# A fused graph, attention and expert kernel on one core: a fourth last group into the output, denominators copied out by ScalarE, x in halves and idle transposes at the start

## The chip, the cores and the metric

The kernel runs on one core of one Trainium2 chip. The metric is the device time of one execution in microseconds (us); lower is better. A core has five engines with a queue each: TensorE (PE in the profile, its weight loads PEld), VectorE (DVE), ScalarE (ACT), GpSimd (POOL) and SyncE (SP), and DMA engines that all queues share. Each engine works its own list of instructions in order and waits on semaphores for the others.

## The reference

With x of 4096 tokens by 256 features and a dense 4096 by 4096 matrix adj, all in float32, cut to what matters:

```python
h = layernorm(x)
x = x + concat([h, (adj @ (h @ neigh_W.T)) / (adj.sum(1) + 1)]) @ lin_W.T
f = layernorm(x)
q, k, v = rope(rmsnorm(f) @ wq.T), rope(rmsnorm(f) @ wk.T), rmsnorm(f) @ wv.T   # 4 heads, 2 kv heads
f2 = f + softmax(causal(q @ k.T / 8)) @ v @ wo.T
flat = rmsnorm(f2)
w = top-2 of softmax(flat @ router_w.T), scaled to sum 1                          # 8 experts
x = x + f2 + sum_e w[:, e] * (silu(flat @ w1[e].T) * (flat @ w3[e].T)) @ w2[e].T
```

## The kernel before, in words

The tokens lie in 8 blocks (`NB`) of 4 tiles (`TB`) of 128. There are three stages, and the order of the instructions on each engine is the order in which the program writes them.

**Graph stage** (L217 to L528). Block 0 of x is loaded first (L238), then the weights `neigh_w` and half of `lin_t` on SP's queue (L241, L242), with the other half on ACT's (L245), then more of x and the first blocks of adj. `scales_x(0)` takes mean and variance of the block (`stats`, L153: four `bn_stats`, four `bn_aggr` on VectorE) and the inverse deviation (`power`, L161: two POOL operations). `normed_x` normalizes one tile on VectorE (L172). `fold` (L279) multiplies the two weights on TensorE into `ml_sb`; `turned_x(0)` transposes the block on TensorE (L319), and `features(0)` (L386) multiplies the two. Then `aggregate` runs over the blocks of adj (L424), with features and later q, k, v as steps in between.

**Attention stage** (L532 to L1337). The list `runs` (L1276) goes over blocks in `ORDER`, two head pairs p, and four key tiles at a time. A run has two places for other work, `place_for_steps(2n)` after the next run's scores and `place_for_steps(2n + 1)` after its own values. `scores` puts two products into one of three PSUM pairs of banks, and ScalarE takes the exponential (L561). `totals` sums the probabilities on VectorE (L579), and `values` multiplies them by v (L591). When a block and head pair is done, `unload` copies the accumulator by ScalarE (L598), and `normalize` (L600) sums over keys by a product with ones into `den`, takes the reciprocal on VectorE (L609) and multiplies (L610). `den` lies in the pool `p_ms`, which has one bank: the next user of it (`project` L625, `turn` L644, `logits`, `weigh`, `place`, `rotate` of the last block) waits until it is read. `at` (L1279) gives each step that needs this bank a place of its own, noted in `taken`; steps that begin with None share a place. For each `normalize` the place after it is put into `taken` as well (L1301). `after(b)` (L800) lists what follows a block: projection, transposes, router, and scatters of its rows into `lists` by expert.

**Expert stage** (L1339 to L1354). Tokens are sorted by expert into 25 whole groups of 256 rows (`NW`) and small groups of 128, of which 17 always run: 42 in all (`NM`). `TURNS` (L55) sets their order: nine whole ones, then whole and small interleaved, then the last `LAST` whole ones. In iteration k: `hidden(k)` (L1176), the load `load13(k + 3)`, `combine(k - 1)`, then `load_rows(k + 4)` and `load2(k + 2)`, all loads on SP. From k = 6, whole groups but the last two are combined by seven smaller products (L1147), for which `split` (L1102) prepares sums of the hidden units and of `w2` on VectorE. Each half of a group is added to its tokens' rows by an indirect DMA with addition from POOL (L1248): into `acc_dram` for the first groups, into `out` for the last `LAST`. At k = NM - LAST, SP copies `acc_dram` into `out` (L1349); it waits for all adds into `acc_dram`, and the adds into `out` wait for it. Adds of different groups into one tensor wait for each other. `load_rows(k + 4)` reuses the buffer of group k - 1 and so waits for that group's add.

Of the kernel before, what the change touches and what calls it, by code (L numbers as in the profile page):

```python
# [9 lines left out]
F32 = mybir.dt.float32  # L10
# [3 lines left out]
ALU = mybir.AluOpType  # L14
# [3 lines left out]
P = 128  # L18
N = 4096
C = 256  # L20
NB = 8
TB = 4
# [9 lines left out]
EPS_LN = 1e-5  # L32
# [16 lines left out]


ALONE = 9
LAST = 3
RARE = 4
NM = NG - RARE
TURNS = list(range(ALONE)) + [  # L55
# [1 line left out]
        ((g - first + 0.5) / (end - first), g)  # L57
        for first, end in ((ALONE, NW - LAST), (NW, NM)) for g in range(first, end)
    )
] + list(range(NW - LAST, NW)) + list(range(NM, NG))  # L60
PADS = 512 + SM
# [5 lines left out]
def fast_kernel(  # L67
# [24 lines left out]
    nc = tc.nc  # L92
# [4 lines left out]
    ident = const.tile([P, P], F32, name="ident")  # L97
# [20 lines left out]
    half = const.tile([P, TB, 1], F32, name="half")  # L118
    nc.gpsimd.memset(half, -0.5)
    experts = const.tile([P, TB, NE], F32, name="experts")  # L120
    for e in range(NE):
# [15 lines left out]
    res = [  # L137
        res_all[:, b * TB * C : (b + 1) * TB * C].rearrange("p (t c) -> p t c", t=TB)
        for b in range(NB)
    ]  # L140
# [5 lines left out]
    mv = [const.tile([P, TB, 2], F32, name=f"mv{b}") for b in range(NB)]  # L146
    rstd = [const.tile([P, TB, 1], F32, name=f"rstd{b}") for b in range(NB)]
    both = [const.tile([P, TB, 1], F32, name=f"both{b}") for b in range(NB)]

    x_blocks = x.rearrange("(b t p) c -> b p t c", t=TB, p=P)  # L150
    out_blocks = out.rearrange("(b t p) c -> b p t c", t=TB, p=P)

    def stats(pool, b):  # L153

        st = pool.tile([P, TB, nc.vector.BN_STATS_DIM], F32, tag="st", name=f"st_{b}")
        for t in range(TB):
            nc.vector.bn_stats(st[:, t, :], res[b][:, t, :])
        for t in range(TB):
            nc.vector.bn_aggr(mv[b][:, t, :], st[:, t, :])

    def power(dst, src, scale, eps):  # L161

        nc.gpsimd.tensor_scalar(dst, src, scale, eps, op0=ALU.mult, op1=ALU.add)
        nc.gpsimd.tensor_tensor(dst, dst, half, op=ALU.pow)

# [4 lines left out]
    def normed(dst, b, t, scale):  # L170

        nc.vector.tensor_scalar(  # L172
            dst, res[b][:, t, :], mv[b][:, t, 0:1], scale, op0=ALU.subtract, op1=ALU.mult
        )
# [42 lines left out]
    with (  # L217
# [11 lines left out]
        def load_x(b):  # L229
            nc.sync.dma_start(res[b], x_blocks[b])  # L230

        def load(n):

            if n < NB * NB:
                blocks[n] = adjs.tile([P, TB, 512], F32, tag="a", name=f"a_{n // NB}_{n % NB}")
                nc.sync.dma_start(blocks[n], adj[n // NB, n % NB])

        load_x(0)  # L238

        wn_sb, l2_sb = qT[4][:, :, 0:C], qT[5][:, :, 0:C]  # L240
        nc.sync.dma_start(wn_sb, neigh_w.rearrange("(c p) o -> p c o", p=P))  # L241
        nc.sync.dma_start(l2_sb, lin_t[C : 2 * C, :].rearrange("(c p) o -> p c o", p=P))  # L242

        ml_sb = qT[6]
        nc.scalar.dma_start(  # L245
# [33 lines left out]
        def fold():  # L279
            for c in range(2):  # L280
                pm = p_pj.tile([P, 512], F32, tag="pj", name=f"pm_{c}")
                for k in range(2):
                    nc.tensor.matmul(
                        pm[:, :C], wn_sb[:, k, c * P : (c + 1) * P], l2_sb[:, k, :],
                        start=(k == 0), stop=(k == 1),
                    )
                nc.scalar.copy(ml_sb[:, c, 0:C], pm[:, :C])
# [43 lines left out]

        inputs, turned = {}, {}

        def scales_x(b):
            stats(gx, b)
            power(rstd[b], mv[b][:, :, 1:2], 1.0, EPS_LN)
            nc.gpsimd.memset(g[b][:, G22 : T1 + 1, :, HC : HC + 1], 1.0)

        def normed_x(b, t):
            if t == 0:  # L340
                inputs[b] = gx.tile([P, TB, C], F32, tag="f", name=f"f_{b}", bufs=1)
            normed(inputs[b][:, t, :], b, t, rstd[b][:, t])
# [119 lines left out]
        def qkv(b):  # L462
# [3 lines left out]
            def scales():  # L466
                stats(gx, b)
                var = mv[b][:, :, 1:2]
                power(both[b], var, *BOTH)
                power(rstd[b], var, 1.0, EPS_LN)  # L470
# [33 lines left out]

        scales_x(0)
        for t in range(TB):
            normed_x(0, t)
        fold()  # L510
        load(2)
        for b in range(6, NB):
            load_x(b)
        scales_x(1)
        turned_x(0)
        features(0)
        turned_x(1)
        scales_x(2)
        steps = {jb: [] for jb in range(NB)}
        for jb in range(NB):  # L520
# [11 lines left out]
    with (  # L532
# [67 lines left out]
        def normalize(b, p):  # L600
            den = p_ms.tile([P, 512], F32, tag="ms", name=f"dn_{b}_{p}")
            total = sums.pop((b, p))
            for j in range(2):
                nc.tensor.matmul(
                    den[j * HD : (j + 1) * HD, :], ones[:, 0:HD], total[:, j, :],
                    start=True, stop=True,
                )
            rden = ax.tile([P, 512], F32, tag="rden", name=f"rden_{b}_{p}")
            nc.vector.reciprocal(rden, den)  # L609
            nc.vector.tensor_mul(ys[b, p], ys[b, p], rden)  # L610


# [210 lines left out]
        def last_qkv():  # L823
            b, made = NB - 1, {}

            def scales():
                stats(ax, b)
                var = mv[b][:, :, 1:2]
                power(rstd[b], var, 1.0, EPS_LN)
                power(both[b], var, *BOTH)  # L830
# [370 lines left out]
        def combine(k):  # L1201
# [33 lines left out]
            for h in range(n):  # L1235
# [6 lines left out]
                else:  # L1242
# [5 lines left out]
                put = nc.gpsimd.indirect_dma_start(  # L1248
                    out=(acc_dram if k < NM - LAST else out)[:, :],
                    out_offset=at,  # L1250
# [26 lines left out]
        later, taken = {}, set()  # L1277

        def at(n, steps):  # L1279

            for fs in steps:
                if fs[0] is None:
                    fs = fs[1:]
                else:
                    while n in taken:
                        n += 1
                    taken.add(n)
                later.setdefault(n, []).extend(fs)
                n += 1
            return n  # L1290
# [6 lines left out]
        ends = {}  # L1297
        for n, (b, p, s) in enumerate(runs[:-1]):
            if s == TB * b:
                ends[b, p] = at(2 * n + 3, [[lambda b=b, p=p: normalize(b, p)]])  # L1300
                taken.add(ends[b, p])  # L1301
        at(0, last_qkv())
        end = 0
        for b in ORDER[:-1]:
# [7 lines left out]
        for n, (b, p, s) in enumerate(runs):  # L1312
# [15 lines left out]


        rest = [[lambda: normalize(ORDER[-1], 1)]] + after(ORDER[-1]) + [  # L1330
            [lambda: make_table(NB, True, NA, NW - NA)], [lambda: make_table(NB, False, NW, NG - NW)],
        ]
        rest = iter([fs for fs in ([f for f in fs if f] for fs in rest) if fs])

        def step():
            for f in next(rest, []):
                f()  # L1337

        load13(2)  # L1339
        for k in range(NM):  # L1340
# [4 lines left out]
            if k:  # L1345
                combine(k - 1)
                step()
            if k == NM - LAST:
                nc.sync.dma_start(out, acc_dram[0:N, :])  # L1349
# [656 lines left out]
@with_exitstack  # L2006
def adj_ffn_kernel(ctx: ExitStack, tc: tile.TileContext, *args):
    nc = tc.nc
    kept = ctx.enter_context(tc.tile_pool(name="kept", bufs=1))
    left_over = kept.tile([1, 1], I32, name="left_over")  # L2010
    table = kept.tile([P, 2, RARE], I32, name="rare_table")
    mine = kept.tile([P, RARE, NE], F32, name="rare_mine")
    lists = fast_kernel(tc, *args, left_over, table, mine)
    state = nc.values_load(left_over[0:1, 0:1], min_val=0, max_val=2)
    with tc.If(state != 0):  # L2015
        with tc.If(state == 2):
            general_kernel(tc, *args)
# [76 lines left out]
```

## Time and profile before

| | |
|---|---|
| median of 3 runs | 1620.64 us (1619.17 to 1621.63) |
| profiled execution | 1620.5 us span |
| graph stage | 0 to about 555 us |
| attention stage | about 555 to 1105 us |
| expert stage | about 1105 us to the end |
| VectorE busy, 580 to 1020 us | 358.0 of 440 us |
| ScalarE busy, 580 to 1020 us | 226.8 of 440 us |
| last product of TensorE ends | 1606.4 us |

In the profile, L12 is line 12 of the program before. A line of a timeline gives the start, the duration, the engine, the line, the operation, what is written and read, the count, and in brackets how long the engine idled before it and what ended that. A q behind an engine's name means its sequencer, such as one that issues a DMA. TensorE is busy nearly all the time, so the places where it isn't are what to look at:

```profile
0.00:20.00 20.00, 12.50 (x38) 1.00 0.94 329
...
700.00:800.00 100.00, 98.01 (x501) 1.00 0.06 22
800.00:900.00 100.00, 97.39 (x494) 1.00 0.09 33
900.00:1000.00 100.00, 99.81 (x483) 1.00 0.08 28
```

These are stretches of the span with TensorE's busy time in each (the columns: stretch, length, busy time and count, granted clock, share of the DMA engines, GB/s).

### The profile page before, as it was taken

What the parts mean: (1) busy time and instruction counts of PE and PEld (TensorE: products, weight loads), DVE (VectorE), ACT (ScalarE), POOL (GpSimd) and SP (SyncE); (2) the same over time, 40 slices, a digit from 0 to 9 for tenths busy, and PEclk for the clock granted to TensorE, in tenths of its full rate; (3) what the DMA queues carried; (4) which work ended last, traced back from release to release, by engine and by line L of the source; (5) the groups of instructions that cost most, each with busy time, mean ns of one, the idle gap of its engine ahead of it and who ended that gap; (6) DMA issues with size and microseconds to landing.
All of it is one profiled execution on the core that took longest, in us unless ns stands there. A gap on an engine that the chain in (4) does not pass through costs nothing. (4 is left out here: it accounts for less than half of the span.)

```text
span 1620.5 us, 25640 instructions
## 1 busy us (share of the span) xinstructions
PE 1592.0 (98%) x9894; PEld 1159.0 (72%) x9894; DVE 1014.8 (63%) x2135; ACT 480.9 (30%) x917; POOL 403.4 (25%) x604
## 2 busy tenths in 40 slices
PE   8999999999999999999999999999999999999996
PEld 5779999999999544344343433437889999999995
DVE  5656756756665678778878888793445444443541
ACT  2110100100100445555454455553212222222221
POOL 1001111112112230443434323322422212222222
PEclk9999999999999999999999999999999999999998
DMA  6324434444444000000001000057756777777775
GB/s 227 97 75 142 157 131 160 138 139 148 160 134 134 4 0 1 24 31 28 35 20 40 28 13 28 17 186 230 236 165 200 240 231 243 251 244 215 242 238 149
DMA packets 67716, 209.79 MB, mean 129 GB/s; under 512 B 14656, under 2 KB 46272, under 8 KB 53952
## 3 DMA queue, kind: packets, MB, share of 16 engines
q1 hardware_dynamic: 54592, 190.32, 34.7%
q0 software_dynamic: 12720, 17.47, 5.4%
q8 instruction: 80, 1.31, 0.3%
q14 instruction: 52, 0.43, 0.1%
q10 hardware_dynamic: 272, 0.26, 0.0%
HBM read 180.81 MB, written 31.42 MB: 131 GB/s over the span
## 5 line engine op out<-in xcount | busy, mean ns | idle before, releaser
L561 ACT ACTIVATE pt<-sc 128x1024 f32<-128x1024 f32 (+3 forms) x288 | 251.6, 958 | 201.3 <-PE sc L556 167.1
L579 DVE TENSOR_TENSOR sum<-sum,pt 128x1024 f32<-128x1024 f32 (+3 forms) x258 | 293.7, 1138 | 20.6 <-POOL pt L563 0.5
L424 PE MATMUL acc<-g,a 128*128 128x128 f32 x2048 | 255.7, 275 | 0.0
L556 PE MATMUL sc<-qT_all,kT 64*128 64x512 f32 (+3 forms) x1152 | 251.4, 570 | 2.8 <-ACT pt L561 1.9
L591 PE MATMUL ya<-pt,vv 128*64 128x512 f32 (+3 forms) x1152 | 242.6, 563 | 0.0
L424 PEld LDWEIGHTS acc<-g,a 128*128 128x128 f32 x2048 | 241.8, 192 | 0.0
L1176 PE MATMUL h<-xT,qT_all 128*128 128x256 f32 (+1 forms) x1232 | 216.6, 335 | 0.0
L1176 PEld LDWEIGHTS h<-xT,qT_all 128*128 128x128 f32 x1232 | 193.4, 191 | 19.0 <-issue 1.0
L556 PEld LDWEIGHTS sc<-qT_all,kT 64*128 64x128 f32 x1152 | 103.5, 186 | 138.2 <-issue 103.0
L1183 DVE TENSOR_TENSOR hT<-si,h 128x256 f32<-128x256 f32 (+2 forms) x126 | 62.6, 506 | 190.6 <-ACT si L1182 190.5
L591 PEld LDWEIGHTS ya<-pt,vv 128*64 128x64 f32 x1152 | 76.3, 136 | 145.4 <-issue 139.3
L1248 POOL DMA_INDIRECT acc_dram<-y,rows x61 | 96.1, 1575 | 332.2 <-DVE y L1243 158.8
L1182 ACT ACTIVATE si<-h 128x256 f32<-128x256 f32 (+2 forms) x126 | 57.0, 453 | 275.9 <-PE h L1176 271.1
L1176 PE MATMUL h<-xT,res_all 128*128 128x256 f32 (+1 forms) x616 | 112.8, 342 | 0.0
L1176 PEld LDWEIGHTS h<-xT,res_all 128*128 128x128 f32 x616 | 99.9, 191 | 10.2 <-issue 0.2
L424 PE MATMUL acc<-g,more_sums 128*128 128x129 f32 (+1 forms) x768 | 101.7, 275 | 0.6 <-DVE more_sums L377 0.6
L424 PEld LDWEIGHTS acc<-g,more_sums 128*128 128x128 f32 x768 | 94.6, 192 | 7.5 <-issue 7.5
L783 POOL DMA_INDIRECT lists<-row,slots x64 | 68.9, 1077 | 114.6 <-issue 111.7
L424 PE MATMUL acc<-g,qT_all 128*128 128x128 f32 (+1 forms) x512 | 74.0, 274 | 0.0
L424 PEld LDWEIGHTS acc<-g,qT_all 128*128 128x128 f32 x512 | 66.5, 192 | 7.2 <-issue 7.2
L198 POOL TENSOR_TENSOR ro<-ro,r 128x192 f32<-128x192 f32 x28 | 16.5, 588 | 218.7 <-DVE r L195 218.7
L563 POOL TENSOR_SCALAR_AFFINE_SELECT pt<-pt 128x256 f32<-128x256 f32 x64 | 39.1, 634 | 127.7 <-ACT pt L561 126.9
(260 smaller groups left out, 1919.4 us busy)
## 6 DMA issues: line engine op xcount, KB each, us to landing
a<-in_adj_dram SPq DMA_DIRECT2D x64, 1024.0 KB, 4.9
qT_all<-in_w_dram SPq DMA_DIRECT2D x28, 1408.0 KB, 8.6
res_all<-in_w_dram SPq DMA_DIRECT2D x28, 768.0 KB, 4.7
res_all<-in_w_dram SPq DMA_DIRECT2D x14, 1408.0 KB, 8.8
qT_all<-in_w_dram SPq DMA_DIRECT2D x14, 768.0 KB, 5.1
rows<-lists SPq DMA_DIRECT2D x25, 265.0 KB, 2.9
lists<-pad SPq DMA_DIRECT2D x8, 662.5 KB, 13.8
res_all<-in_x_dram SPq DMA_DIRECT2D x8, 512.0 KB, 9.0
```

The source lines that it names most:

```text
L198: nc.gpsimd.tensor_sub(ro[:, :, 0, :], ro[:, :, 0, :], r2[:, :, 0, :])
L424: nc.tensor.matmul(acc[t][bank][:, at : at + w], m[left][:, k, t * P : (t + 1) * P], g[jb][:, right, k, 0:w], start=(jb == 0 and k == 0 an ...
L556: nc.tensor.matmul(ps[:, j, :w], kT[sb][hd, i * P : (i + 1) * P], qT[b][hd, p, off:], start=True, stop=True,)
L561: nc.scalar.activation(pt[:, :, :w], ps[:, :, :w], AF.Exp, scale=HD ** -0.5)
L563: nc.gpsimd.affine_select(out=pt[:, :, 0:P], in_=pt[:, :, 0:P], pattern=[[0, 2], [1, P]], compare_op=ALU.is_ge, fill=0.0, base=0, channel_ ...
L579: nc.vector.tensor_add(sums[b, p][:, :, off:], before[:, :, off:], pt[:, :, : 512 - off])
L591: nc.tensor.matmul(accs[b, p][hd, off:], vv[sb][:, i, hd], pt[:, j, : 512 - off], start=(s == 0), stop=(s == TB * b + TB - 1),)
L783: put = nc.gpsimd.indirect_dma_start(out=lists[:, :], out_offset=bass.IndirectOffsetOnAxis(ap=chosen[b][:, k, t, :], axis=0), in_=flats[b] ...
L1176: nc.tensor.matmul(ps[:, m % 2, m // 2 - q, :], w13_sb[:, c, m * P : (m + 1) * P], xT[:, c, :], start=(c == 0), stop=(c == 1),)
L1182: nc.scalar.activation(si[:, 0:both, :], ps[:, 0, 0:both, :], AF.Silu)
L1183: nc.vector.tensor_mul(hT[:, q : q + both, :], si[:, 0:both, :], ps[:, 1, 0:both, :])
L1248: put = nc.gpsimd.indirect_dma_start(out=(acc_dram if k < NM - LAST else out)[:, :], out_offset=at, in_=y[:, h, :], in_offset=None, comput ...
```

## The change

It has three parts.

- `LAST` becomes 4. `TURNS` then holds one whole group less in its interleaved part, which begins at place 9, and one more at the end. The interleaved part has 17 small groups with 12 whole ones instead of 13, and so four pairs of neighbouring small groups instead of three. The copy of `acc_dram` is issued one iteration earlier, and four groups add to `out`.
- `den` is copied to SBUF by ScalarE and the reciprocal is taken in place. The place after each `normalize` is no longer kept free, so the steps behind it move forward.
- The first block of x comes as two DMAs, with statistics and inverse deviation taken for two tiles at a time. `l2_sb` is loaded on ACT's queue instead of SP's. 26 transposes of the identity into an unread PSUM tile stand ahead of `fold` on TensorE.

```diff
-LAST = 3
+LAST = 4
...
-    def stats(pool, b):
+    def stats(pool, b, tiles=range(TB)):
...
-        for t in range(TB):
+        for t in tiles:
             nc.vector.bn_stats(st[:, t, :], res[b][:, t, :])
-        for t in range(TB):
+        for t in tiles:
             nc.vector.bn_aggr(mv[b][:, t, :], st[:, t, :])
...
-        load_x(0)
+        for h in range(2):
+            some = slice(h * TB // 2, (h + 1) * TB // 2)
+            nc.sync.dma_start(res[0][:, some], x_blocks[0][:, some])
...
-        nc.sync.dma_start(l2_sb, lin_t[C : 2 * C, :].rearrange("(c p) o -> p c o", p=P))
+        nc.scalar.dma_start(l2_sb, lin_t[C : 2 * C, :].rearrange("(c p) o -> p c o", p=P))
...
-        def scales_x(b):
-            stats(gx, b)
-            power(rstd[b], mv[b][:, :, 1:2], 1.0, EPS_LN)
+        def scales_x(b, at_a_time=TB):
+            for t in range(0, TB, at_a_time):
+                some = slice(t, t + at_a_time)
+                stats(gx, b, range(TB)[some])
+                power(rstd[b][:, some], mv[b][:, some, 1:2], 1.0, EPS_LN)
...
-        scales_x(0)
+        scales_x(0, TB // 2)
         for t in range(TB):
             normed_x(0, t)
+
+        idle = p_pj.tile([P, TB, P], F32, tag="pj", name="idle")
+        for n in range(26):
+            nc.tensor.transpose(idle[:, n % TB], ident, ident)
         fold()
...
-            nc.vector.reciprocal(rden, den)
+            nc.scalar.copy(rden, den)
+            nc.vector.reciprocal(rden, rden)
             nc.vector.tensor_mul(ys[b, p], ys[b, p], rden)
...
                 ends[b, p] = at(2 * n + 3, [[lambda b=b, p=p: normalize(b, p)]])
-                taken.add(ends[b, p])
```

More of the change, by code (lines that the diff above doesn't have):

```diff
@@ L151, in fast_kernel @@
     out_blocks = out.rearrange("(b t p) c -> b p t c", t=TB, p=P)
-    def stats(pool, b):
-        st = pool.tile([P, TB, nc.vector.BN_STATS_DIM], F32, tag="st", name=f"st_{b}")
-        for t in range(TB):
+    def stats(pool, b, tiles=range(TB)):
+        st = pool.tile([P, TB, nc.vector.BN_STATS_DIM], F32, tag="st", name=f"st_{b}_{tiles[0]}")
+        for t in tiles:
             nc.vector.bn_stats(st[:, t, :], res[b][:, t, :])
-        for t in range(TB):
+        for t in tiles:
             nc.vector.bn_aggr(mv[b][:, t, :], st[:, t, :])
@@ L163, in power @@
         nc.gpsimd.tensor_scalar(dst, src, scale, eps, op0=ALU.mult, op1=ALU.add)
-        nc.gpsimd.tensor_tensor(dst, dst, half, op=ALU.pow)
+        nc.gpsimd.tensor_tensor(dst, dst, half[:, 0 : dst.shape[1]], op=ALU.pow)
     BOTH = (1.0 + EPS_RMS, EPS_LN * EPS_RMS)
```

## The prediction

> **What bounds the kernel now.** I read the page first, then the chain of waits that ended last, then the timeline of each end of the span engine by engine, then the vector engine's reciprocals.
>
> ```profile
> PE 1592.0 (98%) x9894; PEld 1159.0 (72%) x9894; DVE 1014.8 (63%) x2135; ACT 480.9 (30%) x917; POOL 403.4 (25%) x604
> ```
>
> TensorE idles 28.5 of 1620.5 us. Its timeline says where: 7.2 us before its first product, 14.1 us after its last (1606.4), some 5.8 us in the attention stage (555 to 1105) and 1.4 us elsewhere. A change that takes no products away can win only there. First the end: the timeline of POOL, TensorE and the DMA queue (columns: start, duration, engine, line, operands, idle before and what ended it).
>
> ```profile
> 1555.95 1.57 POOL L1248 DMA_INDIRECT acc_dram<-y,rows  x1 [7.84 <-DVE gt L1212]
> ...
> 1566.50 1.57 POOL L1248 DMA_INDIRECT acc_dram<-y,rows  x1 [8.87 <-issue]
> ...
> 1579.95 1.57 POOL L1248 DMA_INDIRECT acc_dram<-y,rows  x1 [9.89 <-DVE hT L1183]
> ...
> 1583.70 0.62 SPq L1349 DMA_DIRECT2D out_dram<-acc_dram  x1
> 1584.57 0.36 SPq L1061 DMA_DIRECT2D res_all<-in_w_dram  x1
> ...
> 1599.62 1.57 POOL L1248 DMA_INDIRECT out_dram<-y,rows  x1 [17.98 <-DMA out_dram<-acc_dram]
> ...
> 1603.66 2.75 PE L1228 MATMUL ye_y<-res_all,hT 128*128 128x256 f32 x12
> ...
> 1606.21 1.57 POOL L1248 DMA_INDIRECT out_dram<-y,rows  x1 [3.04 <-DVE y L1243]
> ...
> 1612.66 1.57 POOL L1248 DMA_INDIRECT out_dram<-y,rows  x1 [2.89 <-DMA out_dram<-y,rows]
> ...
> 1614.54 1.57 POOL L1248 DMA_INDIRECT out_dram<-y,rows  x1 [0.19 <-issue]
> ```
>
> Adds go one group at a time, each waiting for the one before to land. The copy (L1349) waits for the last add into acc_dram, takes 15.1 us to land, and three groups' adds queue behind it, 6.6 and 6.45 us apart. So the copy sets the end, not TensorE. The start:
>
> ```profile
> 5.62 1.41 DVE L157 BATCH_NORM_STATS2 st<-res_all 128x6 f32<-128x256 f32 x4 [5.62 <-DMA res_all<-in_x_dram]
> 7.23 3.75 PE L283 MATMUL pm<-qT_all 128*128 128x256 f32 x8 [7.23 <-DMA qT_all<-in_lin_t_dram]
> 8.75 1.38 DVE L172 TENSOR_SCALAR f<-res_all,mv,rstd 128x256 f32<-128x256 f32 x4 [1.45 <-POOL rstd L164]
> 10.78 1.16 PE L319 MATMUL tr<-ident,f 128*128 128x128 f32 x8
> 12.18 2.41 PE L386 MATMUL pf<-qT_all 128*128 128x512 f32 x5 [0.24 <-ACT qT_all L324]
> ```
>
> The weights' fold (L283) and the first normalized block both end near 10.5. In attention:
>
> ```profile
> L609 DVE RECIPROCAL rden<-dn x16: 3348/3356/3358, 585.1 to 1103.7; 128x512 f32<-128x512 f32 x16
> ...
> 863.29 1.99 PE L625 MATMUL po<-wo_sb,yT 128*128 128x256 f32 x8 [1.36 <-DVE rden L609]
> ```
>
> The reciprocal reads the single spare PSUM bank for 3.36 us, and once TensorE waits for it.
>
> [...] fold products start 0.43 us apart, those of the same 256 columns later 0.215 (L1176), and the transposes at 11 us, 3.6 us after the first product, are already 0.11 apart. [...] the weights issued behind the copy land 16.3 us after issue, 2.1 after the copy. [...] 3356 ns against 693 for the multiply of the same size (L610)[...].
>
> **The change, part by part.**
>
> *Start.* The new transposes need only the identity, written by 1.36. At 0.21 us cold, 26 take 5.5 us; if they warm after 3.6 us, 17 x 0.21 + 9 x 0.11 = 4.6. They end at 6.1 to 7.0, before the weights, whose bytes (1.28 MB of x, two weights and a third) don't change: the fold still starts at 7.2. Warm it takes 8 x 0.215 = 1.7, so transposes may start at 8.95 rather than 10.78. The block: half of x lands earlier, the other half between 5.6 (as the whole before) and 6.2 (an estimate), since lin_t on ACT's queue now shares the engines with it. Two stats, two aggregates, POOL's two operations (1.3), two normalizations (0.7): from 6.2, 0.7 + 0.2 + 1.35 + 0.7 = 9.2, for the last two transposed pairs. So the products of L386 start at about 10.3, 1.7 to 1.9 sooner. After that TensorE runs without gaps over 0.64, so it carries. The extra work (one more DMA issue of 0.5 on SP, two more POOL operations, 1.25) lies in waits. I take -1.7; ends 0 (clock not warmed, or block a, needed at 16.66, now 1.7 sooner, lands too late) and -2.2.
>
> *Denominators.* ScalarE copies 128x512 from PSUM in 0.585 (L598), 16 x 0.585 = 9.4 us on an engine at 51% in that stage; it stands after the values' products, where ScalarE is idle, and only the next exponentials (0.96 each) queue behind it, for whose PSUM banks TensorE's later scores wait. The bank is free 0.6 us after the product instead of 3.4 or more. Hidden: TensorE is working on scores. With the reserved step gone, 15 steps move one place forward: 7 of these successors (rotate 3, project of blocks 3, 4 and 5, place of 3 and 0, weigh of 0) need the bank and the vector engine, which is then still in 3.36 + 0.69 us of reciprocal and multiply. A place is 3.7 us of scores or values, plus its own 2, so it has 1.6 to 2 us to spare. The gain: the 1.36 us wait goes, and some of two waits of 0.66 and 1.04 on L629. begin_experts keeps its place (the last block's steps didn't move). I take -1.5; ends -3 and, below as a rival, a loss.
>
> *Last groups.* One more whole group goes to the end: ...W s W s W W W becomes ...s W s W W W W. The copy moves ahead of the last but one w2 load too, so two loads queue on SP behind its wait. I keep TensorE's end at 1606.4 and go back by its rows: hidden of a whole group 9.94, seven products 4.69, combine of a small one 2.59. The small group before the four then begins to combine at 1554.2. Its y comes 6.7 later (1568.79 to 1575.47 before), at 1560.9. The adds now run late: the last s ready at 1553.1 is added at 1555.95, the W ready at 1560.2 at 1566.50. With a lag of 2.5: add 1563.4, landing after 9.9 (1555.95 to the row load it releases at 1565.89), copy issued 1573.6, landed 1588.7, first add 1589.5, and four groups at 6.53: the last starts at 1609.1 instead of 1612.66. That is -3.6. Hidden: the two w2 loads land 2 and 4.3 us after the copy, 1590.7 and 1593.0, needed at 1595.5 and 1601.0. Bounds: with no lag the add lands in 6 (1381.53 to 1387.48), the copy at 1582.4, and the last product binds: its second add 0.7 after 1606.4 instead of at 1614.54, -7.4. With twice the lag (5.3) it is -0.9; with 8, +1.8.
>
> Sum: -1.7 - 1.5 - 3.6 = -6.8 of the profiled span 1620.5, or 1613.7. That span stands 0.1 under the median of the runs, so 1613.7 serves for both.
>
> **Rivals.**
>
> *No lag at the end.* Lag is what two small groups in a row leave: they take TensorE 2 x 7.9 us, the late chain of adds 2 x 11.1 (1511.00 to 1566.50 are five groups). Of three such pairs before, the first two had healed by 1388.61 and 1442.17, where a whole group was added as soon as its y was there, and only the third's stayed. If it heals: 1620.5 - 1.7 - 1.5 - 7.4 = 1609.9.
>
> *Deeper lag.* The new order has four pairs, nearer together. One that meets a chain already 6.3 late at the whole group ahead of it leaves 6.3 + 2 x 11.1 - 23.3 = 5.2 at its second small group, instead of 2.5 (23.3 is TensorE's own time between these two, 1313.62 to 1336.95, where both were added when ready). Against it: a whole group takes TensorE 14.6 us, which heals. Then 1620.5 - 1.7 - 1.5 - 0.9 = 1616.4, up to 1619 for 8.
>
> *VectorE becomes the bound (slower).* At the seven places above, turn or project waits for a bank whose release is queued behind the reciprocal. If the backlog on arrival exceeds the 2 us to spare by 2 us, 7 x 2 = 14 us: 1620.5 + 14 - 5.3 = 1629; it outweighs the rest from 0.8 us a place. For: the engine is 80% busy there and the wait at 863.29 came from a reciprocal 4.2 us late. Against: the wait for the denominators (24.8 us in 9 of 16) shows it mostly idle on arrival.
>
> *The start doesn't do it.* Idle transposes end late or leave the clock cold: 1615.4.
>
> **How the numbers follow.** Forecast 0.40 (1611 to 1616); no lag 0.27; deeper lag 0.18, of it 0.04 under 1617.4; VectorE 0.09; start idle 0.06. A difference of 0.2%, 3.2 us, is about what can be told from none: faster below 1617.4, slower above 1623.9. Faster 0.40 + 0.27 + 0.04 + 0.05 = 0.76; same 0.14; slower 0.10. The range runs from 1608 (no lag, best ends) to 1619 (8 of lag) and leaves out the slow case and the edges, 0.2.
>
> **What would show it.** The first L386 product near 10.3 and fold products 0.215 apart; no wait on L609 at L625, and waits in attention under 4.5 us in all; the copy issued near 1567 to 1574 with four groups of adds behind it; TensorE's end near 1603. Wrong if the copy lands after 1592 on the old clock, if TensorE's idle time in attention passes 9 us, or if the seven products wait for w2.

## The result, and the profile after

The kernel after took **1614.88 us** (median of 6 executions, 1614.07 to 1617.6) against 1620.23 for the kernel before beside it (6 executions, 1619.12 to 1621.63): a ratio of **0.9972, 95% interval 0.9959 to 0.9984**. It is faster, by 0.3%. The profiled execution of after spans 1613.6 us, that of before 1620.5, a difference of 6.9.

First the page of after: the busy times, and the chain of work that ended last, as shares of the span.

```profile
PE 1596.8 (99%) x9920; PEld 1162.6 (72%) x9920; DVE 1012.8 (63%) x2135; ACT 490.2 (30%) x933; POOL 413.0 (26%) x606
...
PE 95%; DVE 2%; ACT 1%; DMA 0%; POOL 0%; issue 0%; SPq 0%; DVEq 0%; POOLq 0%; ACTq 0%
```

TensorE's count grew by the 26 transposes, and the chain that ends last is now TensorE's own nearly throughout. Before its first real product and after its last one things moved as follows. The end, in the timelines of POOL, SP's queue and TensorE after:

```profile
1537.62 1.57 POOL L1257 DMA_INDIRECT acc_dram<-y,rows  x1 [8.86 <-DVE y L1252]
...
1559.96 1.57 POOL L1257 DMA_INDIRECT acc_dram<-y,rows  x1 [9.93 <-DVE y L1252]
...
1567.22 0.61 SPq L1357 DMA_DIRECT2D out_dram<-acc_dram  x1
1568.08 2.00 SPq L1070 DMA_DIRECT2D res_all<-in_w_dram  x2
...
1583.51 1.57 POOL L1257 DMA_INDIRECT out_dram<-y,rows  x1 [21.87 <-ACT vv L1163]
...
1589.98 1.57 POOL L1257 DMA_INDIRECT out_dram<-y,rows  x1 [2.91 <-ACT si L1191]
...
1597.89 1.57 POOL L1257 DMA_INDIRECT out_dram<-y,rows  x1 [4.35 <-DVE y L1252]
...
1602.11 2.75 PE L1237 MATMUL ye_y<-res_all,hT 128*128 128x256 f32 x12
...
1605.52 1.57 POOL L1257 DMA_INDIRECT out_dram<-y,rows  x1 [3.35 <-DVE y L1252]
1607.39 1.57 POOL L1257 DMA_INDIRECT out_dram<-y,rows  x1 [0.18 <-issue]
```

Read what ends the idle time in the brackets. In before the three groups added into `out` followed the copy 6.6 and 6.45 us apart, each held by the one before; here the last two groups are released by `y` (L1252), the result of the last products. The last add into `acc_dram` too waits for `y` and no longer runs late. TensorE ends at 1604.86, 1.55 sooner than before, and from there to the end of the span it is 8.76 us instead of 14.1: **-1.55 and -5.3 make the -6.9**. The start:

```profile
1.42 4.82 PE L517 MATMUL idle<-ident 128*128 128x128 f32 x26 [1.42 <-POOL ident masks.py:199]
7.16 1.97 PE L285 MATMUL pm<-qT_all 128*128 128x256 f32 x8 [0.91 <-DMA qT_all<-in_neigh_w_dram]
8.96 1.04 PE L321 MATMUL tr<-ident,f 128*128 128x128 f32 x8
10.23 3.27 PE L390 MATMUL pf<-qT_all 128*128 128x512 f32 x7 [0.24 <-ACT qT_all L326]
```

The fold takes 1.97 us instead of 3.75, and the first features product starts at 10.23 instead of 12.18. These 1.95 us are carried unchanged through the graph stage. So TensorE enters attention 1.95 ahead, and ends only 1.55 ahead: something was lost on the way. Attention after, in the timelines of VectorE, ScalarE and TensorE:

```profile
707.97 3.35 DVE L618 RECIPROCAL rden<-rden 128x512 f32<-128x512 f32 x1 [7.67 <-ACT rden L617]
711.36 0.69 DVE L619 TENSOR_TENSOR yT<-yT,rden 128x512 f32<-128x512 f32 x1
711.97 3.60 DVE L587 TENSOR_TENSOR sum<-sum,pt 128x1024 f32<-128x1024 f32 x4
715.49 0.18 DVE L696 TENSOR_TENSOR r_p<-lg,ss 128x32 f32<-128x32 f32 x1
...
716.15 0.23 ACT L705 ACTIVATE r_p<-r_p 128x32 f32<-128x32 f32 x1 [2.01 <-DVE r_p L699]
...
717.35 0.49 PE L564 MATMUL sc<-qT_all,kT 64*128 64x128 f32 x4 [1.71 <-ACT pt L569]
717.77 5.35 PE L599 MATMUL ya<-pt,vv 128*64 128x512 f32 x16
```

The waits of 1.36, 1.04 and 0.66 us for `po` are gone, but a new one of 1.71 stands at 717.35. Follow it back: the score product waits for an exponential (L569); that one stands on ScalarE behind the small exponential of `choose(0)` (L705); this waits for `weigh(0)` on VectorE (L696 to L699), which queues behind the reciprocal of block 4, the multiply and four sums. Then the 16 products at 717.77 take 5.35 us. The same stretch in windows (columns: stretch, length, TensorE's busy time and count, granted clock, share of the DMA engines, GB/s) tells why:

```profile
716.00:718.00 2.00, 0.65 (x6) 1.00 0.00 0
718.00:720.00 2.00, 2.00 (x8) 0.62 0.00 0
720.00:722.00 2.00, 2.00 (x6) 0.53 0.00 0
722.00:724.00 2.00, 2.00 (x12) 1.00 0.00 0
```

After the wait the granted clock is 0.62 and 0.53 in two windows: 2 x 0.38 + 2 x 0.47 = 1.7 us of work at full clock are lost. With that, attention gave no gain in this execution: TensorE's waits there add up to 4.56 us (5.9 before), but it leaves the stage only 1.16 us ahead of before, 0.8 less than it came in with. The other 0.4 of the 1.55 at its end come from the expert stage: from the last product of attention to the last of all it takes 507.45 us, in before 507.84.

### The profile page after: what moved, and what is told of

Read it like the earlier page. It is cut to its first block, busy times and chain, and to the rows that moved or that the text cites. A ratio compares the mean times of both kernels' runs of the same rounds, so it can differ in the third digit from the quotient of the medians.

```text
span 1613.6 us, 25682 instructions
## 1 busy us (share of the span) xinstructions
PE 1596.8 (99%) x9920; PEld 1162.6 (72%) x9920; DVE 1012.8 (63%) x2135; ACT 490.2 (30%) x933; POOL 413.0 (26%) x606
## 4 chain that ended last, share of the span: by engine, by line
PE 95%; DVE 2%; ACT 1%; DMA 0%; POOL 0%; issue 0%; SPq 0%; DVEq 0%; POOLq 0%; ACTq 0%
PE acc L428 25%; PE h L1185 20%; PE ya L599 14%; PE sc L564 13%; PE ye_y L1237 5%; PE pf L390 3%; PE pq L184 3%; PE ye_y L1156 3%; PE ye_ms L1156 2%; PE po L634 2%; DVE sum L587 1%; ACT pt L569 1%; PE tx L1094 1%; PE dn L612 1%; PE tr L321 1%; PE trq L212 1%
## 5 line engine op out<-in xcount | busy, mean ns | idle before, releaser
L569 ACT ACTIVATE pt<-sc 128x1024 f32<-128x1024 f32 (+3 forms) x288 | 251.5, 957 | 155.7 <-PE sc L564 118.6
L1185 PE MATMUL h<-xT,qT_all 128*128 128x256 f32 (+1 forms) x1232 | 225.8, 342 | 0.0
L1185 PEld LDWEIGHTS h<-xT,qT_all 128*128 128x128 f32 x1232 | 200.0, 191 | 21.2 <-issue 1.0
L1257 POOL DMA_INDIRECT acc_dram<-y,rows x59 | 92.9, 1574 | 316.7 <-DVE y L1252 187.8
L1185 PE MATMUL h<-xT,res_all 128*128 128x256 f32 (+1 forms) x616 | 103.6, 327 | 0.0
L792 POOL DMA_INDIRECT lists<-row,slots x64 | 72.7, 1136 | 114.7 <-issue 112.2
L1185 PEld LDWEIGHTS h<-xT,res_all 128*128 128x128 f32 x616 | 93.2, 191 | 8.0 <-issue 0.2
L618 DVE RECIPROCAL rden<-rden 128x512 f32<-128x512 f32 x16 | 53.6, 3350 | 24.3 <-ACT rden L617 24.2
```

What stands on the lines that cost most here:

```text
L569: nc.scalar.activation(pt[:, :, :w], ps[:, :, :w], AF.Exp, scale=HD ** -0.5)
L792: put = nc.gpsimd.indirect_dma_start(out=lists[:, :], out_offset=bass.IndirectOffsetOnAxis(ap=chosen[b][:, k, t, :], axis=0), in_=flats[b] ...
L1185: nc.tensor.matmul(ps[:, m % 2, m // 2 - q, :], w13_sb[:, c, m * P : (m + 1) * P], xT[:, c, :], start=(c == 0), stop=(c == 1),)
L1257: put = nc.gpsimd.indirect_dma_start(out=(acc_dram if k < NM - LAST else out)[:, :], out_offset=at, in_=y[:, h, :], in_offset=None, comput ...
```

## The experiments

All times below are medians; "before" is the kernel before, measured beside it on the same chip. e1 to e4, e5 to e8 and e9 to e12 ran on three different chips. "Tail" is the time from TensorE's last product to the end of the span. Two quantities are read from each profile for the end:

| kernel | median, us | before beside it | ratio, 95% interval | copy issued ahead of TensorE's end | tail |
|---|---|---|---|---|---|
| before | 1620.23 | | | 22.7 | 14.1 |
| after | 1614.88 | 1620.23 | 0.9959 to 0.9984 | 37.6 | 8.8 |
| e1 start alone | 1617.66 | 1619.92 | 0.9980 to 0.9994 | 26.4 | 10.9 |
| e2 four last groups alone | 1617.90 | 1619.92 | 0.9987 to 1.0006 | 34.4 | 9.5 |
| e3 denominators alone | 1620.28 | 1619.92 | 0.9994 to 1.0011 | 26.5 | 10.2 |
| e4 copy by ScalarE alone | 1620.71 | 1619.92 | 0.9996 to 1.0014 | 26.5 | 10.1 |
| e5 freed places alone | 1623.90 | 1619.61 | 1.0012 to 1.0032 | 26.5 | 10.5 |
| e6 after, no idle transposes | 1621.11 | 1619.61 | 0.9994 to 1.0019 | 33.1 | 10.7 |
| e7 after, one place kept free | 1612.97 | 1619.61 | 0.9935 to 0.9970 | 31.0 | 12.1 |
| e8 after, more row buffers | 1614.15 | 1619.61 | 0.9949 to 0.9977 | 41.0 | 8.5 |
| e9 as e7 and e8 together | 1612.26 | 1620.04 | 0.9932 to 0.9965 | 41.1 | 8.4 |
| e10 before, more row buffers | 1619.29 | 1620.04 | 0.9987 to 1.0001 | 26.5 | 12.0 |
| e11 as e8, no idle transposes | 1616.02 | 1620.04 | 0.9963 to 0.9986 | 41.2 | 8.6 |
| e12 as e8, five last groups | 1614.00 | 1620.04 | 0.9946 to 0.9974 | 55.7 | 8.3 |

### The three parts alone

**e1, the start.** All of the edits to the start in the kernel before, nothing else.

> Only the start is changed: x in halves, l2_sb on ScalarE's queue, 26 idle transposes. Theory (the parts add, each in its own stage): the first product of features starts at 10.2 instead of 12.18 us, as in the changed kernel, all later work follows 1.95 us earlier, the copy and the adds at the end as before; span 1618.6. Rival (the adds at the end set the time and run on their own clock of about 11 us a group): the 1.95 us are lost at the end, span 1620.3.

Measured: 2.3 us less than before by the medians (20 executions). The features start 2.0 us sooner (10.17), and TensorE ends at 1604.02, 2.4 sooner than before. The gain at the start is real, and it carries to the end.

**e2, the last groups.**

```diff
-LAST = 3
+LAST = 4
```

> Only LAST = 4. Theory: TensorE's end stays at 1606.4 and the stretch from there to the end of the span shrinks from 14.1 us to about 8.8 as in the changed kernel, if the small group ahead of the last four is added when its y is ready; span 1615.2. Rival (lag stays in the chain of adds, as the forecast took it): copy issued 12.5 us later than that y minus its landing, stretch 10.5, span 1616.9. No gain at all (1620.5) if the changed kernel's shorter end came from the earlier start.

Measured: 1617.9, 2.0 less by the medians; but one of the 12 executions took 1625.55, and the interval of the ratio takes in no change. In the profile the copy is issued at 1571.92 and the tail is 9.5. The copy and the adds behind it still set its end, with the four groups 6.5 us apart, the last two shown here:

```profile
1601.50 1.57 POOL L1248 DMA_INDIRECT out_dram<-y,rows  x1 [2.98 <-DMA out_dram<-y,rows]
...
1608.04 1.57 POOL L1248 DMA_INDIRECT out_dram<-y,rows  x1 [2.98 <-DMA out_dram<-y,rows]
```

**e3, the denominators.** The copy by ScalarE with the reciprocal in place, and the reserved places given up.

> Only the denominators: ScalarE copies them and no place is kept free behind them. Theory (the changed kernel's trace: two waits of 1.36 and 1.04 us at the projection are gone, but choose of block 0 right behind weigh holds ScalarE, and TensorE waits 1.7 us and then runs 3.4 us at half clock): TensorE's end 0.8 us later than before, span 1621.3. Rival (the forecast: 1.5 us gained): span 1619.0. Second rival (the half clock of 3.4 us in the changed trace was chance): the 1.7 us wait shows without it, span 1619.6.

Measured: no gain, +0.4 by the medians with an interval on both sides of 1. The waits of TensorE in its profile:

```profile
PE sc L556 <- ACT pt L561: 3.0, 3, 1.7
PE po L626 <- DVE row L630: 1.4, 1, 1.4
```

The wait for the reciprocal is gone, but the 1.7 for `choose(0)` has come and a wait for `row` has grown to 1.4. In all, TensorE gains 0.55 in attention. The wait came without the half clock here, as the second rival has it: attention takes 559.1 us from its first score product to its last product of the values, as in e8, whose windows after the wait show 1.00. The profiles of e1, e3 and e4 also show that **the profile of before was not a typical one**: with the same three last groups they issue the copy 26.4 to 26.5 us ahead of TensorE's end, not 22.7, and their tails are 10.1 to 10.9, not 14.1. That profile's execution took 1622.21 us, longer than all six of before beside after and all 47 beside e1 (up to 1621.42). The late chain of adds that the prediction read from it is there in some executions only. The three parts alone add up to -3.9 by their medians (-2.3, -2.0, +0.4), against -5.35 for the whole; the intervals of the three reach over 1 us each way, and no run says more on the difference.

### Why the denominators gave nothing

**e4, the copy without the freed places.**

```diff
-            nc.vector.reciprocal(rden, den)
+            nc.scalar.copy(rden, den)
+            nc.vector.reciprocal(rden, rden)
```

> Only the copy by ScalarE; the place behind each denominator is kept free, so every step stands where it stood before. Theory (the places, not the copy, cost): the wait of 1.36 us on the reciprocal goes, the 1.71 us wait of the changed kernel doesn't appear; TensorE idles 4.4 instead of 5.8 us in attention, span 1619.1. Rival (the copy itself delays the exponentials behind it): waits of TensorE on exponentials rise above the 1.9 us of before, span 1620.5 or more.

Measured: 0.8 more than before by the medians, unclear. Neither theory holds: TensorE idles 6.2 us in attention, and its waits for exponentials stay at 1.9. In the timeline of TensorE the wait of 1.36 at 863 is gone, and the next one, 1.04 in before, has become

```profile
871.05 2.42 PE L626 MATMUL po<-wo_sb,yT 128*128 128x256 f32 x8 [2.32 <-DVE row L630]
```

Both waits of before hung on VectorE's queue: taking the bank away from the reciprocal moved the wait one step on, because the work that the bank's next user needs stands in the same queue. The total for `po` is 3.4 (3.1 before). After the 2.32 these 8 products take 2.42 us instead of 1.99 in before, and the 16 of the values behind them 3.59 instead of 2.37. I read that as the half clock again; 1.65 us of this execution's time are that.

**e5, the freed places without the copy.**

```diff
                 ends[b, p] = at(2 * n + 3, [[lambda b=b, p=p: normalize(b, p)]])
-                taken.add(ends[b, p])
```

> The kernel before with the reserved places given up but no copy by ScalarE, so the reciprocal still reads the PSUM bank; 15 steps stand one place earlier. Theory A (the copy is what makes the freed places safe): the 7 steps that need the bank (rotate 3, project of blocks 3, 4, 5, place of 3 and 0, weigh of 0) find it held until the reciprocal ends; each waits 0.5 to 2.5 us of TensorE, TensorE's idle time in attention goes from 5.9 to 10 us or more, and the run takes 1623 to 1632 us. Rival B (VectorE's queue sets these waits, not the bank, as the run with the copy alone suggested): idle time in attention stays at 5 to 7 us and the run takes 1620 to 1621 us, as with both edits together.

Measured: 1623.9, **slower** by 0.22%; theory A by the time, at its low end. But TensorE's idle time in attention was 7.5 us and not the 10 or more that it named. TensorE's waits:

```profile
PE pl L738 <- DVE rden L609: 2.5, 1, 2.5
PE sc L556 <- ACT pt L561: 2.4, 3, 1.2
PE po L625 <- DVE rden L609: 1.8, 2, 1.0
```

`place` of block 3 (L738) waits for the bank until the reciprocal ends, and after that wait the granted clock is 0.80, 0.50 and 0.84 in the three windows of 2 us from 730 to 736, 1.7 us lost. Two projects wait for it as well. So the two edits belong together: freeing the places costs some 3.5 us (1.0022 of 1620) unless the copy makes the bank free, and the copy then buys that back and no more (e3). Which part of the difference e5 makes is bank and which half clock was not separated further.

**e7, one place kept free in after.** The step behind `normalize` of block 4 and head pair 1 moves back by one place, so that `weigh(0)` and `choose(0)` come later.

```diff
+                if (b, p) == (4, 1):
+                    taken.add(ends[b, p])
```

> The kernel after with one single place kept free again, that behind normalize of block 4 and head pair 1, so that weigh of block 0 and choose of block 0 stand one place later. Theory A (the wait of 1.71 us at 717 comes from choose's exponential, which stands in ScalarE's queue behind a reciprocal on VectorE, and the half clock after it follows from that wait): the wait and the half clock are gone, the last product ends 1.7 us (no half clock in the run compared) to 3.4 us sooner, 1611.5 to 1613 us. Rival B (VectorE's backlog just moves on, as it did in the run with the copy alone): a wait of 1 to 2 us appears at another step before 760 us and the time is that of the kernel after, 1614.9 us.

Measured: 1612.97 (four executions: 1612.28, 1612.51, 1613.42 and 1616.65, the last one profiled). TensorE's waits in it:

```profile
PE sc L564 <- ACT pt L569: 1.9, 3, 0.6
...
PE po L634 <- DVE row L638: 1.0, 1, 1.0
```

The 1.7 is gone and no window of attention shows a clock under 1.00. A wait of 1.0 for `row` stands at 749, so B has its share, but TensorE ends at 1602.81, 2.05 sooner than in after although it had begun 0.2 later. So the place given to `choose(0)` did cost the kernel after time. The profiled execution is still long for another reason, the chain of adds, which comes below.

How much each edit of the denominators is worth can be read from all the profiles together, without the spread of whole executions: from TensorE's first score product to its last product of the values the stretch is the same to 0.1 us wherever the code of attention and the clock are the same.

| attention | clock | profiles | stretch, us |
|---|---|---|---|
| as in before | full | before, e1, e2, e10 | 559.6 |
| copy alone | half once | e4 | 561.6 |
| freed places alone | half once | e5 | 563.1 |
| copy and freed places | full | e3, e8, e11, e12 | 559.1 |
| copy and freed places | half once | after, e6 | 560.4, 559.3 |
| copy and freed places, one place kept | full | e7, e9 | 557.3 |

So at full clock the two edits are worth 0.5 us, and 2.3 with the one place kept: the place of `choose(0)` costs 1.8. The half clock costs 1.3 more in after and 0.3 in e6. It doesn't cost its whole 1.7, because the wait of 1.4 us for `row` that follows in e3, e8, e11 and e12 isn't there in after and e6.

### What the idle transposes are worth

**e6, after without them.**

```diff
-        idle = p_pj.tile([P, TB, P], F32, tag="pj", name="idle")
-        for n in range(26):
-            nc.tensor.transpose(idle[:, n % TB], ident, ident)
```

> The kernel after without the 26 idle transposes; x still comes in halves and l2_sb on ACT's queue. Theory A (the gain at the start is the warm clock, the halves only keep it from being lost): the fold's products start 0.43 us apart and end near 10.6, the first features product is at 11.8 to 12.2 instead of 10.23, and the run takes 1.6 to 1.9 us more than the kernel after, 1616.6 us. Rival B (the halves are the gain): features at 10.9 or before, and at most 0.7 us more, 1615.5 us.

Measured: 1621.11, far more than either theory said, with executions from 1616.11 to 1624.88. The start did as theory A expected (TensorE's timeline): fold 3.58 us, features 1.74 later than after.

```profile
7.28 3.58 PE L285 MATMUL pm<-qT_all 128*128 128x256 f32 x8 [7.28 <-DMA qT_all<-in_neigh_w_dram]
10.70 1.04 PE L321 MATMUL tr<-ident,f 128*128 128x128 f32 x8
11.97 4.56 PE L390 MATMUL pf<-qT_all 128*128 128x512 f32 x10 [0.24 <-ACT qT_all L326]
...
1520.08 1.60 PE L1153 MATMUL ye_y<-res_all,hT 128*128 128x128 f32 x12 [2.50 <-DVE y L1249]
```

The halves of x alone therefore gain little (11.97 against 12.18 in before; the other profiles with the old start have 12.27 to 12.92), and the faster fold (1.97 us behind the idle transposes, 3.58 without them) is the larger part. The last line is new: at 1520 TensorE itself waits 2.5 us, for the buffer `y`, which the late adds hold. That pointed to the chain of adds as the rest of the difference, and to a test.

**e11, the same with two more row buffers** (the edit is shown with e8).

> The kernel after without the idle transposes and with the two more row buffers. Theory A (the 1621.1 us without idle transposes was 1.8 us of cold start and the rest a late chain of adds): first features product at 12.0, median 1615.6 to 1616.4 us, no execution above 1617. Rival B (a cold start costs more than its 1.8 us, through something that the start shifts in attention): 1618 us or more, with copies issued in time.

Measured: 1616.02, seven executions from 1615.70 to 1616.38; theory A. First features product at 12.05. Against e8, which has the transposes (1614.15), they are worth 1.9 us (1.4 if each is set against its own before, since the two ran on different chips). The other 5 us of e6 were the late chain: against e11 its profile loses 3.5 us between attention and TensorE's end (510.9 us there instead of 507.45) and 2.2 in the tail.

### The chain of adds

In after, the load of rows for group k + 4 reuses the buffer of group k - 1, so it waits on SP until the adds of k - 1 have landed, and the loads of weights queue behind it. In the profile of e7 this is what POOL and SP's queue show at the end:

```profile
1551.65 1.57 POOL L1257 DMA_INDIRECT acc_dram<-y,rows  x1 [0.19 <-issue]
...
1560.33 0.38 SPq L1080 DMA_DIRECT2D rows<-lists  x1
1560.85 1.57 POOL L1257 DMA_INDIRECT acc_dram<-y,rows  x1 [7.52 <-issue]
...
1571.77 0.61 SPq L1359 DMA_DIRECT2D out_dram<-acc_dram  x1
...
1600.57 1.57 POOL L1257 DMA_INDIRECT out_dram<-y,rows  x1 [2.92 <-DMA out_dram<-y,rows]
...
1608.89 1.57 POOL L1257 DMA_INDIRECT out_dram<-y,rows  x1 [0.19 <-issue]
```

The landing of the add issued at 1551.65 releases the load and the next add within 0.5 us; that add takes 10.9 us until the copy behind it is issued (1560.85 to 1571.77; 7.3 in after, 1559.96 to 1567.22). The copy comes 31.0 us ahead of TensorE's end instead of 37.6, and the tail is 12.1.

The profiles also show what runs beside that add. The loads of weights behind the load of rows are issued at 1560.96 and 1561.85, beside the add, and the copy is issued 0.2 us after the last of them has landed (1571.55; in e2 1571.70 and 1571.92, in e6 1575.73 and 1575.96). In after, e2, e6 and e7, which have four last groups and the old buffers, the last add into `acc_dram` is issued among such loads and takes 7.3 to 10.9 us until the copy is issued. In the other ten profiles these loads have landed by then, to 0.1 us, and it takes 3.7 to 3.9.

**e8, two more row buffers in after**, taken from a tile that attention no longer needs. From the 12th group on every third group uses them.

```diff
+        more_rows = []
...
-            r = ex.tile([P, HALF, ROW], F32, tag="rows", name=f"rows_{i}", bufs=5)
+            if k >= 12 and k % 3 == 2:
+                if not more_rows:
+                    more_rows.append(ax.tile([P, TB, ROW], F32, tag="row", name="more_rows"))
+                at_row = k // 3 % 2 * HALF
+                r = more_rows[0][:, at_row : at_row + HALF, :]
+            else:
+                r = ex.tile([P, HALF, ROW], F32, tag="rows", name=f"rows_{i}", bufs=5)
```

> The kernel after with two more row buffers for every third group from the 12th on, so that the loads of rows no longer wait for the add of the group just before. Theory A (what is left of the kernel after's spread is the chain of adds that in some executions runs late because loads, adds and copy wait for each other): the copy is issued at 1567 or before in the profile, the executions spread by less than 1 us, and the median is 1613.5 to 1614.3 us. Rival B (the adds wait only for each other's landing, the buffers don't matter): time and spread as for the kernel after, 1614.9 us with 1614 to 1617.6. Rival C: loads issued sooner collide with the adds, which then land later, and the time rises to 1616 us or more.

Measured: 1614.15, five executions from 1613.72 to 1614.49 (1614.07 to 1617.6 for after). The copy is issued at 1562.64, 3.9 us after the last add ahead of it, and the tail is 8.5. Theory A: the long executions are gone. Over e8, e9, e11 and e12, which all have these buffers, 21 executions, no kernel's executions differ by more than 1 us.

**e10, the same in before.**

> The kernel before with only the two more row buffers. Theory A (before too loses time to the late chain of adds in many executions): the copy is issued 26 us or more ahead of the last product's end (22.7 in the profile of before), the median falls from 1619.7 to 1617.8 to 1618.4 us and the executions spread by less than 1.5 us (3.7 to 5.3 before). Rival B (the copy, not the lag, is the cost): 1619.5 us and the spread of before.

Measured: 1619.29 (1617.96 to 1620.75), 0.75 less by the medians and within what can't be told from none. The longest executions of before (to 1623.84 beside it) are gone, and the copy is issued 26.5 us ahead of TensorE's end, as expected; but the spread stays at 2.8 and the tail of the profiled one was 12.0, its adds into `out` being 8.0 us apart once (1602.73 to 1610.72) instead of 6.5. So neither theory holds alone: with three last groups the end hangs on the copy and three adds whatever the chain ahead of it does, and every delay of these shows.

**e12, five last groups.**

```diff
-LAST = 4
+LAST = 5
```

> The kernel after with the two more row buffers and five groups at the end instead of four. Theory A (with four the last product already sets the end, 8.5 to 8.8 us ahead of the end of the span): no more to win, 1613.9 to 1614.6 us, copy issued near 1541 to 1552. Rival B (one more neighbouring pair of small groups, now nearer together, makes the chain of adds late again): 1615 us or more, TensorE waiting for y at L1156. Rival C (adds to out that are no longer pressed): 1612 to 1613.5 us.

Measured: 1614.00, like e8. The copy is issued 55.7 us ahead of TensorE's end instead of 41.0, and the tail shrinks by 0.2 only. With four groups the last product already sets the end. The fourth group was worth the move, a fifth isn't.

**e9, both additions in after.**

> The kernel after with both additions: two more row buffers for every third group, and the one place behind normalize of block 4 and head pair 1 kept free. Theory A (the two act on different things: the wait of 1.71 us in attention, and executions with a late chain of adds): every execution within 1 us of the others, as with the buffers alone, and the median at the undisturbed executions of the one place, 1612.3 to 1612.8 us. Rival B (with the place kept free the executions differ because of the place, not the chain): some executions still at 1616 us, median about 1613 us.

Measured: **1612.26**, four executions from 1612.09 to 1612.59, the best of all kernels here: 0.9949 of before. Its end (POOL and SP's queue):

```profile
1560.79 0.61 SPq L1366 DMA_DIRECT2D out_dram<-acc_dram  x1
...
1576.49 1.57 POOL L1264 DMA_INDIRECT out_dram<-y,more_rows  x1 [17.81 <-DMA out_dram<-acc_dram]
...
1594.93 1.57 POOL L1264 DMA_INDIRECT out_dram<-y,rows  x1 [7.87 <-DVE y L1259]
...
1602.44 1.57 POOL L1264 DMA_INDIRECT out_dram<-y,more_rows  x1 [3.23 <-DVE y L1259]
```

The first add into `out` is still released by the copy, the last ones by `y`: at 6.5 us a group the last one could have started at 1596.1, 6.3 sooner than its `y` let it. Against e8 this is 1.9 less (2.3 if each is set against its own before): the place of `choose(0)` and the chain of adds are two separate costs.

## Why the prediction was right, and where it wasn't

The forecast, 1613.7 with a range of 1608 to 1619, lies 1.2 us from the measured 1614.88, and "faster" was right. Its total for the profiled spans, -6.8, met -6.9, **but by errors that cancel, and that is luck**: for -1.7, -1.5 and -3.6 the profiles have -1.95 at the start, +0.8 in attention and -5.3 in the tail, with -0.4 between attention and TensorE's end that no term stood for.

- **Start, -1.7: right.** Measured -1.95 in after, 2.3 by the medians of e1. Fold products are 0.216 us apart (0.215 forecast), the features start at 10.23 (10.3 forecast), the idle transposes take 4.82 us (4.6 estimated) and end at 6.24. In after the transposes are 0.213 us apart at first and 0.109 from 5.1 us on, 3.7 after the first; in before the transposes are 0.11 apart from 11.1 us on, 3.9 after the first product. In e1 and e8 the 26 transposes took 5.70 and 5.74 us, and the features still started at 10.17 and 10.33. Taking -1.7 of "1.7 to 1.9 sooner" was the cautious end. The rival that the start doesn't do it is ruled out by e1, and e11 shows that the transposes do most of it.
- **Denominators, -1.5: wrong.** Alone they gave +0.4 by the medians; by the stretches above they are worth -0.5 at full clock, and +0.8 in the profile of after with its half clock. The reading that the bank comes free 0.6 us after the product was right, and the copy (0.586 us) didn't raise TensorE's waits for exponentials (1.9 us in e4 as in before). Two steps failed. One is "the 1.36 us wait goes, and some of two waits": the waits go, but e4 shows that what is behind them is VectorE's queue, so they came back elsewhere. The other is the statement that "only the next exponentials (0.96 each) queue behind it": I followed what each moved step needs from the bank and VectorE, and not what it puts on ScalarE. `choose(0)` moves an exponential that waits for VectorE ahead of the exponentials that TensorE's scores need. e7 and e9 show the cost, 1.8 us at full clock. The reciprocal from SBUF takes 3352 ns against 3356 from PSUM, as the forecast counted it (3.36 us).
- **Last groups, -3.6: right in mechanism, mis-sized.** In the two profiles the tail shrank by 5.3. The forecast had the copy issued 32.8 us ahead of TensorE's end (1573.6 to 1606.4); it was 37.6. Of the two terms that the sum carried over from the profile of before, the lag of 2.5 us wasn't there (the last add into `acc_dram` at 1559.96, its `y` ready at 1559.68), and the landing of that add took 7.3 us, not 9.9. The rival *No lag at the end* was nearer, with 39.1 ahead. Against the tails of e1, e3 and e4 (10.1 to 10.9), which have three last groups without the lag, the gain is 1.3 to 2.1. The step that failed is to treat the lag of one profiled execution as a property of the kernel. Both cases exist: e7's profiled execution issued the copy 31.0 us ahead. That rival's own -7.4 was too much: it put the second add of the last group 0.7 us after TensorE's end; that is where the first one goes, and the second is issued 2.5 us after TensorE's end (1604.86 to 1607.39). The sums have small slips that change nothing: 1563.4 + 9.9 is 1573.3, not 1573.6, and the two longer lags give -0.8 and +1.9, not -0.9 and +1.8.
- **"That span stands 0.1 under the median of the runs, so 1613.7 serves for both": wrong.** The time of an execution is 1.7 us above its own span (1622.21 for 1620.5 in before, 1615.35 for 1613.6 in after). The execution profiled in before was thus 1.6 above the median of 1620.64. By medians the change is worth 5.35 us, not 6.9.
- **VectorE becomes the bound (slower): not in after.** None of the seven places waits on the reciprocal there. e5 shows the mechanism when the copy is missing, with 4.3 us of waits at three places instead of 14 at seven.
- **Deeper lag** was not seen in the profile of after. Two of its six executions took 1617.5 to 1617.6, which fits a late chain, but they have no trace.
- Of the marks named ahead: the copy was issued at the early edge of 1567 to 1574 as said; the two w2 loads behind the copy stayed hidden (TensorE's products of L1237, from 1594.34 to its end, follow one another without a wait). TensorE's end was 1604.86 and not 1603, and the waits in attention 4.56 and not under 4.5, both because of the 1.71 at 717.

What stays open: why the chain of adds falls behind in some executions and not in others, and why e6 did so in most of its executions. That more row buffers end it is shown for the kernel after; in before (e10) they end the longest executions, not the spread. That adds are slow beside loads of weights is read from the profiles, not tried by itself.

## What to carry to other kernels

When a step is moved, list what it issues on every engine, and for each of these instructions what it waits for and who stands behind it; the bank that the change is about may not be the queue that decides. Before a wait of one profiled execution goes into a sum, compare that execution's time with the other executions: it may be a wait that only some of them have. A closing transfer with a chain of adds behind it should be issued so early that the last product sets the end; beyond that point an earlier issue was worth nothing here (e12: 0.2 us of the tail).

## What was not expected of the hardware

A wait of TensorE of 1.71 us in after was followed by windows at a granted clock of 0.62 and 0.53 (1.7 us lost), and one of 2.52 us in e5 likewise. The windows of e5 after its wait:

```profile
730.00:732.00 2.00, 1.04 (x6) 0.80 0.00 0
732.00:734.00 2.00, 2.00 (x6) 0.50 0.00 0
734.00:736.00 2.00, 2.00 (x15) 0.84 0.00 0
```

The length of the wait alone doesn't decide it. These are the longest waits of attention in the profiles that have one of 1.7 us or more, and one of e6 in the expert stage:

| profile | wait, us | ends at | after it |
|---|---|---|---|
| e5 | 2.52 | 730.96 | clock 0.50 from 732 to 734 |
| e4 | 2.32 | 871.05 | 16 products take 3.59 us instead of 2.37 |
| e6 | 1.71 | 719.12 | clock 0.63 and 0.52 from 720 to 724 |
| after | 1.71 | 717.35 | clock 0.62 and 0.53 from 718 to 722 |
| e6 | 2.50 | 1520.08 | clock 1.00 from 1520 to 1530 |
| e8 | 1.71 | 717.49 | clock 1.00 from 718 to 724 |
| e11 | 1.70 | before 720 | clock 1.00 from 710 to 730 |
| e12 | 1.71 | before 720 | clock 1.00 from 710 to 730 |
| e3 | 1.7 | in attention | 559.1 us of attention, as in e8 |

The same wait of 1.7 us went both ways, and one of 2.50 us left the clock at 1.00. What decides it was not shown. With four cases of half clock this is what the profiles show, not more. So the half clock in after is a matter of the execution: the six profiles with this attention code all have the wait, and two of them have the half clock.
